# Smaller projection pieces, x prefetched by groups, and partial row sums on VectorE in entry 0 of a two-layer graph attention kernel

## Chip, cores and metric

The kernel runs on one core of a Trainium2 chip. The metric is the device time of one execution in microseconds; the median of several runs is compared.

## What is computed

Eight graphs (entries) of 2,048 nodes with 256 features share one adjacency matrix. Layer 0 is an attention layer with eight heads of 32 features, whose scores are sums of a source and a destination term with a leaky ReLU, plus a logarithmic prior made from the adjacency. Layer 1 is a dot-product attention layer with one head. Each has a residual and a layer norm.

```
# layer 0, per entry
x_proj = einsum('bnd,hdf->bhnf', x, W)
e = leaky_relu(e_src[..., :, None] + e_dst[..., None, :], 0.2)
e = where(adj > 0, e + softplus(beta_tilde) * log(adj + 1e-6), -max)
h = einsum('bhij,bhjf->bhif', softmax(e), x_proj)     # then @ W_out.T
x = layernorm(x + h)
# layer 1
e = where(adj > 0, leaky_relu((x W1)(x W2)^T, 0.2), -1e12)
x = layernorm(x + relu(softmax(e) (x W3)))
```

## The kernel before

**Layer 0 as units.** The exponential of a leaky ReLU of a sum is the larger of two products, so no exponential is taken per score. For one pair of heads (`hp`, 0 to 3) and one tile of 128 keys (`jt`, 0 to 15), a *unit*, `step` (line 295) makes for each of the two heads one tile `s` of 128 keys x 2,048 queries by one VectorE instruction (line 311): the maximum of a query row `c`, broadcast over the partitions, and a per-key number, times the transposed mask `mt`. TensorE then multiplies `s` by the projected values into `val` and by a per-key weight, broadcast to 32 columns, into `den`, the row sums of the softmax (`products`, line 333). `s` has four buffers, that is two units.

**Row sums on VectorE.** `SUMMED` (line 67) lists key tiles whose row sums aren't taken by `den` matmuls. The first of a list is scaled by ScalarE into two tiles `d` (line 324), one for each head; the others are added to them by VectorE (line 318), a unit later in program order; at the last key tile one group of matmuls with ones adds `d` to `den` (line 329). Entry 0's list is empty before the change.

**Entry 0.** Its 64 units run alone, before layer 1 of any entry. In its first pair (units 0 to 15) the masks are made: `make_mt` (line 163) loads a column block of the adjacency as `adj_t`, makes `m` by VectorE (line 168), two ScalarE passes (169, 170) and VectorE again (171), transposes it on TensorE (176), copies it out on ScalarE (177) and stores it as `mt_d`. `m` has the two buffers of tag "p". Masks are made one tile ahead of their unit. The later pairs load `mt` back, with two buffers of tag "mt" and two of tag "d".

**Projections as filler.** Entry 0's own projection comes first. Those of entries 1 to 7 (`project`, line 225) are cut into pieces and put between entry 0's units by the main loop (lines 479 to 483). There are six pieces for each entry: four groups of 512 rows, each with the transposes of the next group ahead of it (`turn`, line 234), one piece for the scaling of the values `v` (line 270, a VectorE instruction of 4,096 elements), and one for `est` (line 277), from which the rows `c` are made. x is loaded in halves of 1 MB into the buffers of tag "p", which the masks use too. `later_weights` (line 133) prepares W_out, W1 W2 and W3, with a buffer of tag "pen".

**The end of a pair.** `finish` (line 341) copies `val` and `den` out on ScalarE, moves one row of each quarter of `den` into `rc` by DMA, takes the reciprocal on VectorE (line 354), stores it, and after each second pair loads it back broadcast as `rb` and multiplies (line 363). Then the output projection (`y`, line 376) can start.

**Order.** TensorE's order is the program's. The other engines' order is chosen by a scheduler at compile time; each then works its queue in that order. All DMAs are issued by SyncE from one queue, also in a fixed order. After entry 0's units, layer 1 of an entry runs together with layer 0 of the next; nothing in the change touches that part.

Of the kernel before, what the change touches and what calls it, by code (L numbers as in the profile page):

```python
# [9 lines left out]
F32 = mybir.dt.float32  # L10
# [8 lines left out]
P = 128  # L19
# [8 lines left out]
def kernel(  # L28
# [26 lines left out]
    nc = tc.nc  # L55
    B, N, D = x.shape
    H, _, DH = w_proj.shape
    NT = N // P
    KC = D // P
    BK = 512  # L60
    NB = N // BK
    HALF = N // 2
    HP = 2
    NP = H // HP
    IG = BK // P

    SUMMED = [(), (1, 3, 6, 9, 12)] + [(1, 3, 6, 8, 11, 13)] * (B - 2)

    const = ctx.enter_context(tc.tile_pool(name="const", bufs=1))
    dram = ctx.enter_context(tc.tile_pool(name="dram", bufs=1, space=DRAM))  # L70
# [1 line left out]
    wide = ctx.enter_context(tc.tile_pool(name="wide", bufs=2))  # L72
# [5 lines left out]
    def mm_tile(name):  # L78
        return ps.tile([P, BK], F32, tag="mm", name=name)

    def wide_tile(name, tag, bufs, dtype=F32):
        return wide.tile([P, N], dtype, tag=tag, name=name, bufs=bufs)
# [6 lines left out]
    ident = const.tile([P, P], F32)  # L89
# [14 lines left out]
    nc.vector.scalar_tensor_tensor(beta[:, 3:4], beta[:, 0:1], 0.0, beta[:, 2:3], ALU.max, ALU.add)  # L104
    beta_c = beta[:, 3:4]

    def load_x(b, half):
        xr = wide.tile([P, NT // 2, D], F32, tag="p", name="xr", bufs=2)
        nc.sync.dma_start(xr, x[b].rearrange("(t p) d -> p t d", p=P)[:, ts(half, NT // 2), :])
        return xr  # L110

    first_x = [load_x(0, half) for half in range(2)]


    wp = const.tile([P, KC, D + 2 * H], F32)
# [17 lines left out]
    def later_weights():  # L133

        nc.sync.dma_start(w3s, w3.rearrange("(k p) d -> p k d", p=P))
        w1t, w2t = (chunk.tile([P, KC, D], F32, tag="pt", name=name, bufs=2) for name in ("w1t", "w2t"))
        for w, dst in ((w_out, wot), (w1, w1t), (w2, w2t)):
            src = wide.tile([P, KC, D], F32, tag="pen", name="square", bufs=1)
            nc.sync.dma_start(src, w.rearrange("(k p) c -> p k c", p=P))
            yield  # L140
            for kc in range(KC):
                t = mm_tile("sq_t")
                for o in range(KC):
                    nc.tensor.transpose(t[:, ts(o, P)], src[:, o, ts(kc, P)], ident)
                nc.scalar.copy(dst[:, kc, :], t[:, 0:D])
        yield
        for dc in range(KC):
            t = mm_tile("w12p")
            for kc in range(KC):
                nc.tensor.matmul(t[:, 0:D], w1t[:, kc, ts(dc, P)], w2t[:, kc, :], start=(kc == 0), stop=(kc == KC - 1))  # L150
            nc.scalar.copy(w12[:, dc, :], t[:, 0:D])
        yield
# [7 lines left out]
    rec_d = dram.tile([B, NP, 4, HALF], F32, name="rec_d")  # L160
    x1_d = dram.tile([B, N, D], F32, name="x1_d")

    def make_mt(jt):

        a = wide.tile([P, NT, P], I32, tag="d", name="adj_t", bufs=2)
        nc.sync.dma_start(a, adj[:, ts(jt, P)].rearrange("(t p) j -> p t j", p=P))
        m = wide.tile([P, NT, P], F32, tag="p", name="m", bufs=2)
        nc.vector.tensor_scalar(m, a, 0.0, None, ALU.max)
        nc.scalar.activation(m, m, AF.Ln, bias=eps_prior)
        nc.scalar.activation(m, m, AF.Exp, scale=beta_c)  # L170
        nc.vector.scalar_tensor_tensor(m, a, 0.0, m, ALU.is_gt, ALU.mult)
        mt = wide_tile("mt", "mt", 2)
        for g in range(NB):
            t = mm_tile("mtp")
            for k in range(IG):
                nc.tensor.transpose(t[:, ts(k, P)], m[:, g * IG + k, :], ident)
            nc.scalar.copy(mt[:, ts(g, BK)], t)
        nc.sync.dma_start(mt_d[ts(jt, P), :], mt)
        return mt
# [32 lines left out]
    def row_tile(name, bufs=4):  # L212
        return small.tile([P, D], F32, tag="row", name=name, bufs=bufs)


    class Gat:


        def __init__(self, b):
            self.b = b  # L220
            self.units = ((hp, jt) for hp in range(NP) for jt in range(NT))
            self.hts = []
            self.mts = []

        def project(self):


            b = self.b
            kept = "v" if b == 0 else ("h3", "x1t")[b % 2]
            self.v = v = whole.tile([P, NT, D], F32, tag=kept, name="v")  # L230
            both = small.tile([P, NT, 2 * H], F32, name="both", bufs=1)
            xrs, xts = [], []

            def turn(g):
                if g % 2 == 0:
                    xrs.append(load_x(b, g // 2) if b > 0 else first_x[g // 2])
                xt = chunk.tile([P, KC, BK], F32, tag="ht", name="xt", bufs=3)
                for kc in range(KC):
                    t = mm_tile("tr")
                    for k in range(IG):  # L240
                        nc.tensor.transpose(t[:, ts(k, P)], xrs[-1][:, g % 2 * IG + k, ts(kc, P)], ident)
                    nc.scalar.copy(xt[:, kc, :], t)
                xts.append(xt)

            turn(0)
            for g in range(NB):
                if g + 1 < NB:
                    turn(g + 1)
                for k in range(IG):
                    it = g * IG + k  # L250
                    t = mm_tile("proj")
                    for kc in range(KC):
                        nc.tensor.matmul(t[:, 0:D + 2 * H], xts[g][:, kc, ts(k, P)], wp[:, kc, :],
                                         start=(kc == 0), stop=(kc == KC - 1))
                    nc.scalar.copy(v[:, it, :], t[:, 0:D])
                    nc.scalar.copy(both[:, it, :], t[:, D:D + 2 * H])
                yield
            top = small.tile([P, 2, H], F32, name="top", bufs=1)
            ed, es = both[:, :, 0:H], both[:, :, H:2 * H]
            nc.vector.tensor_reduce(top[:, 0, :], ed.rearrange("p t h -> p h t"), AX.X, ALU.max)  # L260
            nc.gpsimd.partition_all_reduce(top[:, 1, :], top[:, 0, :], P, bass_isa.ReduceOp.max)
            cs = small.tile([P, H, NT], F32, name="cs", bufs=1)
            nc.vector.tensor_tensor(cs, es.rearrange("p t h -> p h t"),
                                    top[:, 1, :].unsqueeze(2).to_broadcast([P, H, NT]), ALU.add)
            nc.vector.tensor_tensor(ed, ed, top[:, 1:2, :].to_broadcast([P, NT, H]), ALU.subtract)
            self.re = re = small.tile([P, 2, NT, H], F32, name="re", bufs=2)
            nc.scalar.activation(re[:, 0], ed, AF.Exp, scale=-(1.0 - ALPHA))
            nc.scalar.activation(re[:, 1], ed, AF.Exp)
            v4 = v.rearrange("p t (h f) -> p (t h) f", f=DH)
            nc.vector.tensor_tensor(v4, v4, re[:, 1].rearrange("p t h -> p (t h)").unsqueeze(2).to_broadcast(  # L270
                [P, NT * H, DH]), ALU.mult)
            if b > 0:
                nc.sync.dma_start(v_d[b], v)
                nc.sync.dma_start(re_d[b], re)
            yield
            t = mm_tile("est")
            nc.tensor.transpose(t[:, 0:P], cs.rearrange("p h t -> p (h t)"), ident)
            est = row_tile("est")[:, 0:P]
            nc.scalar.activation(est, t[:, 0:P], AF.Exp, scale=1.0 - ALPHA)
            nc.sync.dma_start(c_d[b].rearrange("h (t p) -> (h t) p", p=P), est)  # L280
            yield
# [13 lines left out]
        def step(self, count=1):  # L295

            for _ in range(count):
                hp, jt = next(self.units)
# [3 lines left out]
                    self.den = pacc.tile([P, HALF], F32, tag="den", name="den")  # L302
                first = self.b == 0 and hp == 0
                while first and len(self.mts) < min(jt + 2, NT):
                    self.mts.append(make_mt(len(self.mts)))
                mt = self.mts[jt] if first else load_mt(jt, self.b == 0)
                s = []
                for a in range(HP):
# [3 lines left out]
                    s.append(sa)  # L312
                v, e = self.v, self.re[:, 1]
                heads = [hp * HP + a for a in range(HP)]
                chain = SUMMED[self.b]
                if jt - 1 in chain[1:]:
                    for d, sa, h in zip(self.sums, self.last, heads):
                        nc.vector.scalar_tensor_tensor(d, sa, e[:, jt - 1, h:h + 1], d, ALU.mult, ALU.add)  # L318
                self.last = s
                self.products(self.val, [v[:, jt, ts(h, DH)] for h in heads], s, jt == 0, jt == NT - 1)  # L320
                if jt in chain[:1]:
                    self.sums = [wide_tile("d", "d", 2) for _ in heads]
                    for d, sa, h in zip(self.sums, s, heads):
                        nc.scalar.activation(d, sa, AF.Copy, scale=e[:, jt, h:h + 1])
                if jt not in chain:
# [149 lines left out]
    for _ in gats[0].project():  # L475
        pass
    others = (1 for g in gats[1:] for _ in g.project())
    weights = later_weights()
    pieces = (B - 1) * (NB + 2)
    for k in range(NP * NT):  # L480
        gats[0].step()
        for _ in range((k + 1) * pieces // (NP * NT) - k * pieces // (NP * NT)):
            next(others)
        if k >= NT and k % 4 == 0:
            next(weights, None)
    for _ in others:
        pass


    dot = None  # L490
    for b in range(1, B + 1):
# [53 lines left out]
```

## Time and profile before

| | us |
|---|---|
| median of 3 runs | 4469.75 |
| lowest, highest | 4466.98, 4470.57 |
| span of the profiled execution | 4465.4 |
| PE, DVE, ACT busy in it | 4267.6, 3631.8, 1758.7 |
| entry 0's own projection and first masks | 0 to 41 |
| s of units 0 to 15 (pair 0, masks made) | 53.9 to 209.2 |
| s of units 16 to 63 (pairs 1 to 3) | to 535.1 |
| first output matmul (y) | 559.3 |

PE is TensorE, DVE VectorE, ACT ScalarE, SP SyncE. A group of instructions is given by line, engine, operation and tiles, with its count, its busy time, the mean duration of one in ns, and then the idle time of the engine just before such instructions with the work that ended it. A row of waits reads: engine and line that waited, the engine and line waited for, total, number, longest. Each fp32 matmul appears in the records as two instructions.

### The profile page before, as it was taken

Reading aid. Unit: us, or ns where it says so; the run is one execution under the profiler, and the core shown is the slowest. Engines: PE = TensorE matmul, PEld = TensorE weight load, DVE = VectorE, ACT = ScalarE, POOL = GpSimd, SP = SyncE. Lnnn points to the kernel's source line nnn. Section 1 sums busy time; section 2 is a strip of 40 time slices with the busy share of each in tenths; the row PEclk is TensorE's granted clock in tenths of the full one; section 3 lists DMA queues with packets and bytes.
Section 4 is the critical chain, followed back from the end, with each engine's and each line's share of the span. In section 5 each row is a group of like instructions: output and inputs, shape, how many; then the busy total and the mean of one; then the engine's idle time right before and its main releaser. Section 6 shows DMA issues by size and latency. Waiting matters only on the chain.

```text
span 4465.4 us, 60558 instructions
## 1 busy us (share of the span) xinstructions
PE 4267.6 (96%) x24988; PEld 2217.3 (50%) x24988; DVE 3631.8 (81%) x2605; ACT 1758.7 (39%) x3611; POOL 7.5 (0%) x14
## 2 busy tenths in 40 slices
PE   6899899999999999999999999999999999999899
PEld 4444344445455545555455544545454554554566
DVE  5778798888989988988899888888988888898222
ACT  5622233334333343334333343333433343333555
POOL 0000000000000000000000000000000000000000
PEclk8999999999999999999999999999999999999999
DMA  7777665666555555556555565555545565553211
GB/s 217 262 264 263 249 218 204 220 233 217 180 189 193 182 193 184 188 181 224 176 182 178 186 213 187 189 181 207 194 160 190 189 216 183 187 182 134 69 50 41
DMA packets 252773, 843.62 MB, mean 189 GB/s; under 512 B 33616, under 2 KB 152400, under 8 KB 176976
## 3 DMA queue, kind: packets, MB, share of 16 engines
q1 hardware_dynamic: 252496, 839.74, 54.0%
q8 instruction: 196, 3.21, 0.3%
q14 instruction: 81, 0.66, 0.0%
HBM read 763.76 MB, written 75.37 MB: 188 GB/s over the span
## 4 chain that ended last, share of the span: by engine, by line
PE 60%; DVE 14%; issue 8%; ACT 4%; DMA 1%; SPq 0%; DVEq 0%; ACTq 0%
PE acc L461 17%; PE e L426 15%; PE val L336 12%; DVE s L311 9%; PE den L336 8%; PE pt L445 4%; DVE d L318 3%; PE h1p L416 2%; ACT p L432 1%; PE h3p L396 1%; ACT h L210 1%; DVE p L431 1%; PE y L376 1%; DMA mt<-mt_d 0%; ACT f L206 0%
## 5 line engine op out<-in xcount | busy, mean ns | idle before, releaser
L311 DVE SCALAR_TENSOR_TENSOR s<-c,re,mt 128x2048 f32<-128x2048 f32 x1024 | 2350.6, 2343 | 209.6 <-PE den L336 159.9
L336 PE MATMUL val<-s,v 128*32 128x512 f32 x8192 | 1045.3, 607 | 78.7 <-DVE s L311 78.5
L461 PE MATMUL acc<-h,pts 128*128 128x256 f32 x4096 | 950.6, 380 | 14.9 <-ACT pts L447 14.4
L426 PE MATMUL e<-x1t,h 128*128 128x512 f32 x2048 | 904.0, 594 | 0.0
L461 PEld LDWEIGHTS acc<-h,pts 128*128 128x128 f32 x4096 | 748.2, 190 | 107.7 <-ACT pts L447 21.8
L336 PE MATMUL den<-s,re 128*32 128x512 f32 x5568 | 709.2, 598 | 0.0
L318 DVE SCALAR_TENSOR_TENSOR d<-s,re,d 128x2048 f32<-128x2048 f32 x272 | 632.4, 2343 | 0.0
L426 PEld LDWEIGHTS e<-x1t,h 128*128 128x128 f32 x2048 | 379.6, 190 | 450.1 <-issue 417.9
L336 PEld LDWEIGHTS val<-s,v 128*32 128x32 f32 x8192 | 240.9, 110 | 697.8 <-issue 526.3
L447 ACT COPY pts<-pt 128x512 f32<-128x512 f32 x512 | 296.1, 583 | 664.7 <-PE pt L445 664.4
L428 ACT ACTIVATE p<-e 128x512 f32<-128x512 f32 x512 | 302.5, 595 | 432.3 <-PE e L426 432.3
L431 DVE CUSTOM_DVE_ANT_0 p<-p,pen 128x2048 f32<-128x2048 f32 x128 | 292.7, 2287 | 205.9 <-ACT p L428 205.6
L336 PEld LDWEIGHTS den<-s,re 128*32 128x32 f32 x5568 | 194.2, 112 | 426.7 <-issue 426.6
L432 ACT ACTIVATE p<-p,neg 128x2048 f32<-128x2048 f32 x128 | 256.7, 2005 | 272.5 <-DVE neg L431 272.5
L445 PEld LDWEIGHTS pt<-ident,p 128*128 128x128 f32 x2048 | 238.0, 141 | 223.5 <-issue 167.2
L445 PE MATMUL pt<-ident,p 128*128 128x128 f32 x2048 | 318.7, 279 | 5.4 <-ACT p L432 5.4
L469 DVE TENSOR_TENSOR z<-z,x1r 128x256 f32<-128x256 f32 x128 | 54.0, 422 | 205.4 <-ACT z L468 197.0
L468 ACT ACTIVATE z<-acc,rec 128x256 f32<-128x256 f32 x128 | 60.6, 473 | 355.9 <-PE acc L461 330.3
L376 PE MATMUL y<-wot,ht 128*128 128x256 f32 x512 | 129.6, 414 | 37.4 <-DVE ht L363 36.3
L206 ACT ACTIVATE f<-mv,eps_ln 128x1 f32<-128x1 f32 x256 | 74.2, 290 | 199.0 <-DVE mv L204 198.1
L396 PE MATMUL h3p<-w3s,x1t 128*128 128x256 f32 x512 | 133.4, 386 | 12.3 <-ACT x1t L392 12.3
L376 PEld LDWEIGHTS y<-wot,ht 128*128 128x128 f32 x512 | 104.7, 208 | 68.3 <-DVE ht L363 39.2
(76 smaller groups left out, 2083.6 us busy)
## 6 DMA issues: line engine op xcount, KB each, us to landing
mt<-mt_d SPq DMA_DIRECT2D x496, 1024.0 KB, 4.8
c<-c_d SPq DMA_DIRECT2D x64, 1024.0 KB, 6.7
pen<-pen_d SPq DMA_DIRECT2D x112, 512.0 KB, 3.3
xr<-in_x_dram SPq DMA_DIRECT2D x16, 1024.0 KB, 7.1
adj_t<-in_adj_dram SPq DMA_DIRECT2D x16, 1024.0 KB, 6.8
mt_d<-mt SPq DMA_DIRECT2D x16, 1024.0 KB, 5.6
rb<-rec_d SPq DMA_DIRECT2D x64, 256.0 KB, 4.0
h<-in_x_dram SPq DMA_DIRECT2D x32, 512.0 KB, 5.9
```

The lines of the kernel that those rows point to most:

```text
L311: nc.vector.scalar_tensor_tensor(sa, self.cs[a], self.re[:, 0, jt, h:h + 1], mt, ALU.max, ALU.mult)
L318: nc.vector.scalar_tensor_tensor(d, sa, e[:, jt - 1, h:h + 1], d, ALU.mult, ALU.add)
L336: nc.tensor.matmul(dst[ts(q, DH), ts(c, BK)], weights[q % 2], s[q % 2][:, ds(q // 2 * HALF + c * BK, BK)], start=start, stop=stop)
L376: nc.tensor.matmul(y[:, 0:D], ht[:, ts(it, P)], wot[:, g, :], start=(g == 0), stop=(g == 1))
L396: nc.tensor.matmul(t[:, 0:D], x1t[:, kc, ts(it - 1, P)], w3s[:, kc, :], start=(kc == 0), stop=(kc == KC - 1))
L426: nc.tensor.matmul(t, self.h1[:, kc, ts(it % IG, P)], self.x1t[:, kc, ts(c, BK)], start=(kc == 0), stop=(kc == KC - 1))
L428: nc.scalar.activation(p[:, ts(c, BK)], t, AF.Prelu, alpha=ALPHA)
L431: nc.vector.tensor_tensor_reduce(p, p, pen, -1.0, FMAX, ALU.add, ALU.min, neg)
L432: nc.scalar.activation(p, p, AF.Exp, bias=neg, scale=-1.0, accum_out=den)
L445: nc.tensor.transpose(t[:, ts(k, P)], p[:, ts(g * IG + k, P)], ident)
L447: nc.scalar.copy(pt, t)
L461: nc.tensor.matmul(acc, now[:, ts(k, P)], self.h3[:, j, :], start=(j == 0), stop=(j == NT - 1))
```

## The change

It does four things. Entry 0's pairs 1 to 3 get a list of six summed key tiles. The projection pieces become one row tile of 128 rows each, 18 for each entry, spread over the first 60 of the 64 units, so that the filler is even and ends before the last units. x is loaded in groups of 512 rows (0.5 MB) into the single buffer of tag "pen", each when the transposes of the group before have been queued; a group is thus a group ahead of its use, and tag "p" is left to `m` and, in pairs 1 to 3, to the sums `d`. And `m` is made one tile further ahead of its transposes. The weights' loads move to row buffers.

```diff
-    SUMMED = [(), (1, 3, 6, 9, 12)] + [(1, 3, 6, 8, 11, 13)] * (B - 2)
+    SUMMED = [(1, 3, 6, 8, 11, 13), (1, 3, 6, 9, 12)] + [(1, 3, 6, 8, 11, 13)] * (B - 2)
...
-            src = wide.tile([P, KC, D], F32, tag="pen", name="square", bufs=1)
-            nc.sync.dma_start(src, w.rearrange("(k p) c -> p k c", p=P))
+            src = [row_tile("square") for _ in range(KC)]
+            for o in range(KC):
+                nc.sync.dma_start(src[o], w[ts(o, P), :])
...
+    def x_groups():
+
+        for b in range(1, B):
+            for g in range(NB):
+                xg = wide.tile([P, IG, D], F32, tag="pen", name="xg", bufs=1)
+                nc.sync.dma_start(xg, x[b].rearrange("(t p) d -> p t d", p=P)[:, ts(g, IG), :])
+                yield xg
+
+    groups = x_groups()
+    ahead = []
...
             def turn(g):
-                if g % 2 == 0:
-                    xrs.append(load_x(b, g // 2) if b > 0 else first_x[g // 2])
+                if b == 0:
+                    xr = first_x[g // 2][:, ds(g % 2 * IG, IG), :]
+                else:
+                    xr = ahead.pop() if ahead else next(groups)
...
+                if b > 0:
+                    ahead.extend(xg for xg in [next(groups, None)] if xg is not None)
 
             turn(0)
-            for g in range(NB):
-                if g + 1 < NB:
+            for it in range(NT):
+                g, k = divmod(it, IG)
+                t = mm_tile("proj")
+                for kc in range(KC):
+                    nc.tensor.matmul(t[:, 0:D + 2 * H], xts[g][:, kc, ts(k, P)], wp[:, kc, :],
+                                     start=(kc == 0), stop=(kc == KC - 1))
+                nc.scalar.copy(v[:, it, :], t[:, 0:D])
+                nc.scalar.copy(both[:, it, :], t[:, D:D + 2 * H])
+                if k == 0 and g + 1 < NB:
                     turn(g + 1)
...
                 while first and len(self.mts) < min(jt + 2, NT):
-                    self.mts.append(make_mt(len(self.mts)))
+                    at = len(self.mts)
+                    while len(self.ms) < min(at + 1 + (jt > 0), NT):
+                        self.ms.append(make_m(len(self.ms)))
+                    self.mts.append(make_mt(at, self.ms[at]))
...
-                chain = SUMMED[self.b]
+                chain = () if first else SUMMED[self.b]
...
-                    self.sums = [wide_tile("d", "d", 2) for _ in heads]
+                    self.sums = [wide_tile("d", "d" if self.b else "p", 2) for _ in heads]
...
-    pieces = (B - 1) * (NB + 2)
+    pieces = (B - 1) * (NT + 2)
     for k in range(NP * NT):
         gats[0].step()
-        for _ in range((k + 1) * pieces // (NP * NT) - k * pieces // (NP * NT)):
+        due = [min(i * pieces // (NP * NT - 4), pieces) for i in (k, k + 1)]
+        for _ in range(due[1] - due[0]):
             next(others)
-        if k >= NT and k % 4 == 0:
+        if k >= NT and k % 4 == 2:
             next(weights, None)
-    for _ in others:
-        pass
-
```

More of the change, by code (lines that the diff above doesn't have):

```diff
@@ L105 @@
     beta_c = beta[:, 3:4]
[L107 to L112, printed above, removed]
+    first_x = [wide.tile([P, NT // 2, D], F32, tag="p", name="xr", bufs=2) for _ in range(2)]
+    for half, xr in enumerate(first_x):
+        nc.sync.dma_start(xr, x[0].rearrange("(t p) d -> p t d", p=P)[:, ts(half, NT // 2), :])
     wp = const.tile([P, KC, D + 2 * H], F32)
@@ L143, in later_weights @@
                 for o in range(KC):
-                    nc.tensor.transpose(t[:, ts(o, P)], src[:, o, ts(kc, P)], ident)
+                    nc.tensor.transpose(t[:, ts(o, P)], src[o][:, ts(kc, P)], ident)
                 nc.scalar.copy(dst[:, kc, :], t[:, 0:D])
@@ L161, with make_m @@
     x1_d = dram.tile([B, N, D], F32, name="x1_d")
-    def make_mt(jt):
+    def x_groups():
[6 more added lines that the diff above has]
+    ahead = []
+    def make_m(jt):
         a = wide.tile([P, NT, P], I32, tag="d", name="adj_t", bufs=2)
@@ L171, in make_mt @@
         nc.vector.scalar_tensor_tensor(m, a, 0.0, m, ALU.is_gt, ALU.mult)
+        return m
+    def make_mt(jt, m):
         mt = wide_tile("mt", "mt", 2)
@@ L222, in __init__ @@
             self.hts = []
-            self.mts = []
+            self.ms, self.mts = [], []
         def project(self):
@@ L231, in project @@
             both = small.tile([P, NT, 2 * H], F32, name="both", bufs=1)
-            xrs, xts = [], []
+            xts = []
             def turn(g):
-                if g % 2 == 0:
-                    xrs.append(load_x(b, g // 2) if b > 0 else first_x[g // 2])
+                if b == 0:
+                    xr = first_x[g // 2][:, ds(g % 2 * IG, IG), :]
+                else:
+                    xr = ahead.pop() if ahead else next(groups)
                 xt = chunk.tile([P, KC, BK], F32, tag="ht", name="xt", bufs=3)
@@ L240, in turn @@
                     for k in range(IG):
-                        nc.tensor.transpose(t[:, ts(k, P)], xrs[-1][:, g % 2 * IG + k, ts(kc, P)], ident)
+                        nc.tensor.transpose(t[:, ts(k, P)], xr[:, k, ts(kc, P)], ident)
                     nc.scalar.copy(xt[:, kc, :], t)
                 xts.append(xt)
+                if b > 0:
+                    ahead.extend(xg for xg in [next(groups, None)] if xg is not None)
             turn(0)
-            for g in range(NB):
-                if g + 1 < NB:
-                    turn(g + 1)
[L249 to L256, printed above, removed]
+            for it in range(NT):
[7 more added lines that the diff above has]
+                if k == 0 and g + 1 < NB:
+                    turn(g + 1)
                 yield
```

## The prediction

> **What bounds the kernel now.** The change touches only entry 0's attention. From the first query-product matmul of layer 1 on (633 us) the compiled program queues the same instructions in the same order on all engines, so I read the first 560 us. First the slices of the page, for the shape:
>
> ```profile
> PE   6899899999999999999999999999999999999899
> DVE  5778798888989988988899888888988888898222
> ```
>
> A slice is 111.6 us. In the first five TensorE is less full than later, and VectorE is not full either. Then the busy time by stretch: pair 0, where the masks are built (unit 15's s end at 209.2); pairs 1 to 3 (unit 63's s end at 535.1); the passage into the next stage.
>
> ```profile
> core 0: us, PE busy (x) PEld busy (x) DVE busy (x) ACT busy (x) POOL busy (x), PEclk, DMA share, GB/s
> 41.00:209.00 168.00, 131.72 (x916) 74.68 (x916) 130.12 (x67) 108.92 (x170) 0.36 (x1) 0.91 0.81 260
> 209.00:535.00 326.00, 295.08 (x2057) 131.79 (x2057) 253.92 (x125) 74.16 (x242) 6.03 (x6) 0.96 0.71 256
> 535.00:560.00 25.00, 13.75 (x82) 3.58 (x83) 13.08 (x8) 6.47 (x6) 0.00 (x0) 0.73 0.84 293
> ```
>
> Nobody is saturated in pairs 1 to 3; PE looks nearer the bound, but its 295 us hold cold stretches. The waits of the second stretch say why:
>
> ```profile
> DVE s L311 <- PE den L336: 56.6, 21, 4.4
> DVE s L311 <- PE proj L253: 6.7, 1, 6.7
> DVE s L311 <- DMA c<-c_d: 2.9, 2, 2.6
> ...
> PE val L336 <- DVE s L311: 29.9, 14, 5.2
> ```
>
> Both wait for each other: VectorE some 66 us, TensorE 30. The four s buffers hold two units, and a projection lump is longer than that slack, as PE's timeline shows (start, duration):
>
> ```profile
> 490.11 1.99 PE L241 MATMUL tr<-ident,xr 128*128 128x128 f32 x16
> 491.94 3.93 PE L253 MATMUL proj<-wp,xt 128*128 128x272 f32 x16
> 495.80 1.92 PE L336 MATMUL val<-s,v 128*32 128x512 f32 x16
> 497.54 1.90 PE L336 MATMUL den<-s,re 128*32 128x512 f32 x16
> 499.38 1.09 PE L241 MATMUL tr<-ident,xr 128*128 128x128 f32 x8
> ```
>
> From start to start: four row tiles of projection 3.86, val 1.74, den 1.84, one group's transposes 0.92. What VectorE does in 209.5 to 535.1:
>
> ```profile
> L311 DVE SCALAR_TENSOR_TENSOR s<-c,re,mt 128x2048 f32<-128x2048 f32 x96 | 220.1, 2346 | 66.2 <-PE den L336 56.6 <-PE proj L253 6.7 <-DMA c<-c_d 2.9
> L270 DVE TENSOR_TENSOR v<-v,re 128x4096 f32<-128x4096 f32 x6 | 26.5, 4423 | 2.5 <-ACT re L268 2.5
> L363 DVE TENSOR_TENSOR ht<-ht,rb 128x2048 f32<-128x2048 f32 x1 | 2.3, 2283 | 0.0
> ```
>
> With the four small groups (cs 2.2, top 2.1, both 1.7, rc 1.0) that is 255.9 us of 325.6.
>
> In pair 0 the mask chain costs most: VectorE waits from 63 us on are
>
> ```profile
> DVE s L311 <- ACT mt L177: 13.2, 4, 4.7
> DVE m L168 <- PE mtp L176: 12.2, 4, 3.9
> DVE m L168 <- DMA adj_t<-in_adj_dram: 5.4, 2, 5.1
> ```
>
> **What the Trainium skill says.** (1) "VectorE: DVE Perf Modes", section "The perf-mode tier table": an fp32 operation on two tensors has only the 1x mode, 2,293 ns for 2,048 elements. Lines 311 and 318 agree, 2.29 to 2.35 us; a cheaper add on VectorE isn't to be had. (2) "TensorE: Matmul & The Clock Gate", section "What's actually happening": an array that idled for about 3.4 us runs at half rate. The trace agrees: after a 3 us wait at 292 us eleven val matmuls take 2.78 us, against 1.49 at 535 us. (3) "DMA: Bandwidth & Descriptors", section "Anatomy of one DMA": a semaphore wait happens on the issuing sequencer, not in the DMA engine. So an x load that waits for TensorE holds up mt loads behind it on SyncE; no row of the trace shows such a block by itself.
>
> **Part 1, the row sums.** Per pair six of sixteen tiles lose their den matmuls, and one group with ones comes back: 3 x (6 - 1) x 1.8 = 27 us off TensorE. The first tile of each pair is scaled on ScalarE, 6 x 2.0 = 12 us; it is busy 74 of 326 us, so hidden, but a projection copy can stand behind it for 2 to 4 us. The other five are added on VectorE: 3 x 5 x 2 = 30 adds. The row for this very operation,
>
> ```profile
> L318 DVE SCALAR_TENSOR_TENSOR d<-s,re,d 128x2048 f32<-128x2048 f32 x272 | 632.4, 2343 | 0.0
> ```
>
> gives 632.4/272 = 2.325 us, so 69.7 us. VectorE then needs 255.9 + 69.7 = 325.6 us for a stretch that lasts 325.6 us now. This is the step that carries the forecast: pairs 1 to 3 can't become shorter, and each microsecond of VectorE idleness left in them is lost.
>
> **Part 2, pieces of a row tile.** 126 pieces over 60 units, 2.1 per unit: TensorE's extra per unit is 2.1 x 0.96 + 0.5 x 0.92 = 2.5 us instead of lumps of 4.8. A plain unit then costs it 3.6 + 2.5 = 6.1 us and VectorE 4.6; a summed unit 4.3 against 9.2. Of the 66 us of waits for TensorE the smoothing and the lighter den remove most. What stays, by estimates:
> - Start of a pair (three times): the second c row can't be loaded before the last unit's first s has read its buffer; c lands in 6.7 us (issue table), with two s (4.6 us) to hide it: 2 to 2.9 us, 7 in all.
> - From unit 14 of a pair to unit 3 of the next no add falls due. TensorE has two plain units, the ones, two more plain units and a summed one before VectorE is delayed again, some 29 us against 23, with 4.6 us of lead; and the reciprocal (line 354) stands after two units of the next pair in VectorE's queue, with all later s behind it, and waits for the later-closing den. 3 us twice: 6.
> - x a group ahead with one buffer: at an entry's start turn(0), one projection and turn(1) are one piece. The load for turn(1) goes out when turn(0) has read the buffer, lands in about 6 us (h, same 512 KB, 5.9 in the issue table), and TensorE has 1 us of work: it stands still for 5 us, and val, the next mask transposes and all else on PE behind it. Five times in pairs 1 to 3. VectorE is then a unit ahead and has just got the 4.4 us of v, so it loses from 0 to 5 us, I take 1.2: 6.
> - Cold stretches after such waits: 3.
> Sum 22 us; from 8 (all but the c rows hidden) to 38 (stalls not hidden, mt loads late).
>
> **Part 3, masks one tile deeper (pair 0).** x no longer takes turns with m in the "p" buffers, and m is made a tile further ahead; the 12.2 and part of the 13.2 us go. VectorE's floor per unit is 4.6 + 2.3 + 1.2 = 8.1 us, with v 8.5; ScalarE has 4.0 + 2.3 + 1.7 = 8.0 and TensorE 3.6 + 1.9 + 2.5 = 8.0. Three engines this close won't run at 8.5; I take 9.2, where units 3 to 15 now take 123.4/12 = 10.3: gain 13. Against it: the first piece now lies before the transposes of mask 2, with its 5 us of waiting for x, so unit 3 starts about 4.5 us later (85.7 instead of 81.2), and entry 2's start in unit 9 costs up to 6, taken as 4. Net gain 5 us, from a loss of 5 to a gain of 15.
>
> **Part 4, the passage.** Today
>
> ```profile
> 546.02 0.35 DVE L354 RECIPROCAL rc<-rc 128x32 f32<-128x32 f32 x1 [10.97 <-DMA rc<-dn]
> ```
>
> holds four s of the next entry behind it. The changed queue puts these ahead of the reciprocal, and the last four units carry no projection. VectorE gains 9 us, but the output matmuls still wait for den, rc, rb and the product of line 363, 24 us after unit 63, and den closes 1.9 us later with the ones. I take 3 us, from 0 to 6. The weights' new buffers and slots cost nothing: the same 20 small matmuls (4 us) lie in TensorE's slack.
>
> Sum: 22 - 5 - 3 = +14 us, 4484.
>
> **Rivals.**
> *No change:* stalls are absorbed (8 to 12) and pair 0 gains 8 to 10. For it: TensorE, 295 - 27 = 268 us busy of 326, will have 58 us of slack in pairs 1 to 3 to catch up in. Against: VectorE has none. 10 - 8 - 3 = -1, about 4469.
> *Faster:* pair 0 runs near its floor (-15), the passage gives 5, and pairs 1 to 3 lose only 4: -16, 4454. For it: the 25 us of mask waits are of the kind that one tile more of depth removes. Against: three engines within half a microsecond of one another.
> *Much slower:* SyncE's queue makes mt late after each x load (5 x 3 more), pair 0 gains nothing: 22 + 15 - 2 = +35, 4505.
>
> **Numbers.** Main case 0.42, much slower 0.10, no change 0.28, faster 0.20. Low end 4455, high end 4506. Slower by over 0.2% (8.9 us) takes the first two.
>
> **What would show it.** Over pairs 1 to 3 VectorE should be busy about 325 us in a stretch of 335 to 360; TensorE's waits for s should exceed VectorE's for den. Each entry's turn(1) should show a wait for xg of some 5 us. The reciprocal should wait for its transfer. Unit 3's s should start near 86 us. I am wrong if that stretch is below 333 us, if adds cost less than 2.2 us each, or if pair 0 ends before 195 us.

## The result, and the profile after

The changed kernel takes 4487.03 us (median of 4 runs, 4485.46 to 4488.95) against 4469.22 us: a ratio of 1.0041, 95% interval 1.0023 to 1.0058. It is slower by 17.8 us; 4484 was forecast. The span of the profiled execution is 4487.2 us, 21.8 more than before. Every trace is one execution, and executions of one kernel lie up to 12 us apart here, so a few us between two traces mean little by themselves.

Lines of `kernel.py` have moved: s is line 331 (311 before), the add 338 (318), val and den 356 (336), the transposes of x 257 (241), the reciprocal 374 (354), the product with rb 383 (363). Where the text says "the stretch" of a run, it means pairs 1 to 3, from the end of unit 15's s to the end of unit 63's s. Below, "later turn" means that the transposes of the next x group stand two pieces later.

The slices of the changed kernel's page, PE above DVE:

```profile
PE   6888889999999999999999999999999999999899
DVE  5799998888989988888998888888988888898222
```

VectorE is now at 90% or more in the third to sixth slice, and TensorE has gone down there: the bound has changed sides. The same stretches as before the change (pair 0 and pairs 1 to 3):

```profile
core 0: us, PE busy (x) PEld busy (x) DVE busy (x) ACT busy (x) POOL busy (x), PEclk, DMA share, GB/s
41.00:207.00 166.00, 137.18 (x923) 76.99 (x921) 132.47 (x69) 110.38 (x177) 0.77 (x2) 0.89 0.79 250
207.00:555.00 348.00, 292.47 (x1802) 129.93 (x1800) 319.70 (x155) 86.77 (x249) 11.95 (x6) 0.92 0.71 248
```

Pairs 1 to 3 went from 325.9 to 348.5 us. VectorE's busy time in them rose from 253.9 to 319.7 us, by about 66, and its idle time fell by about 44, from 72 to 28; the balance is the growth of the stretch, 22.6 us. Marks on the way, from VectorE's timeline and the first matmul of layer 1 (h1p):

| | before, us | after, us | difference added |
|---|---|---|---|
| s of unit 0 starts | 53.9 | 56.6 | +2.7 |
| s of unit 15 ends | 209.2 | 207.1 | -4.8 |
| s of unit 63 ends | 535.1 | 555.6 | +22.6 |
| first h1p | 633.3 | 653.4 | -0.4 |
| end | 4465.4 | 4487.2 | +1.7 |

What VectorE did most in pairs 1 to 3 of the changed kernel, by group:

```profile
L331 DVE SCALAR_TENSOR_TENSOR s<-c,re,mt 128x2048 f32<-128x2048 f32 x97 | 222.5, 2342 | 19.3 <-DMA mt<-mt_d 8.8 <-DMA c<-c_d 5.4 <-PE den L356 2.9
L338 DVE SCALAR_TENSOR_TENSOR d<-s,re,d 128x2048 f32<-128x2048 f32 x30 | 69.5, 2343 | 0.0
```

The 56.6 us of waits for den have become 2.9, and 69.5 us of adds have taken their place. The waits there, VectorE's and then TensorE's:

```profile
DVE s L331 <- DMA mt<-mt_d: 8.8, 2, 4.5
DVE s L331 <- DMA c<-c_d: 5.4, 3, 2.6
DVE rc L374 <- DMA rc<-dn: 3.6, 2, 2.6
DVE top L277 <- ACT both L271: 3.6, 3, 2.5
DVE s L331 <- PE den L356: 2.9, 3, 1.7
DVE s L331 <- PE val L356: 2.1, 1, 2.1
...
PE val L356 <- DVE s L331: 23.2, 19, 3.9
PE tr L257 <- DMA xg<-in_x_dram: 17.3, 5, 5.7
PE est L294 <- DVE cs L280: 13.9, 4, 4.1
```

TensorE now waits for VectorE (23.2 and 13.9 us); VectorE's waits for den and val are down to 5.0. The five waits for xg are the starts of the five entries whose projection begins in these pairs: turn(1) has nothing to hide its load behind. In pair 0 TensorE waits for xg twice, 3.0 and 3.1 us, with mask transposes behind it. VectorE's waits from 63 to 207 us:

```profile
DVE m L178 <- PE mtp L190: 23.1, 5, 10.7
DVE s L331 <- ACT mt L191: 3.8, 2, 2.8
```

The waits of s for mt fell from 13.2 to 3.8 us, those of m for the transposes rose from 12.2 to 23.1, of which two, of 10.7 and 10.6 us, lie right after the starts of entries 1 and 2; the later turn (below) halves these waits, to 11.2 us. At the passage

```profile
568.46 0.35 DVE L374 RECIPROCAL rc<-rc 128x32 f32<-128x32 f32 x1 [1.97 <-DMA rc<-dn]
```

comes after four s, where it held them for 10.97 us before.

### The profile page after: what moved, and what is told of

Same layout as the page of the kernel before. It is cut to its first block, busy times and chain, and to the rows that moved or that the text cites. A ratio compares the mean times of both kernels' runs of the same rounds, so it can differ in the third digit from the quotient of the medians.

```text
span 4487.2 us, 60148 instructions
## 1 busy us (share of the span) xinstructions
PE 4272.2 (95%) x24748; PEld 2219.9 (49%) x24748; DVE 3698.2 (82%) x2635; ACT 1772.0 (39%) x3617; POOL 13.4 (0%) x14
## 3 DMA queue, kind: packets, MB, share of 16 engines
q1 hardware_dynamic: 252768, 839.74, 53.9%
## 4 chain that ended last, share of the span: by engine, by line
PE 59%; DVE 15%; issue 8%; ACT 4%; DMA 2%; SPq 0%; DVEq 0%
PE acc L481 16%; PE e L446 15%; PE val L356 11%; DVE s L331 10%; PE den L356 8%; PE pt L465 4%; DVE d L338 3%; PE h1p L436 2%; PE y L396 1%; ACT p L452 1%; PE h3p L416 1%; DVE p L451 1%; ACT h L224 1%; DMA mt<-mt_d 1%; DVE ht L383 0%
## 5 line engine op out<-in xcount | busy, mean ns | idle before, releaser
L338 DVE SCALAR_TENSOR_TENSOR d<-s,re,d 128x2048 f32<-128x2048 f32 x302 | 702.0, 2343 | 0.0
L356 PE MATMUL den<-s,re 128*32 128x512 f32 x5280 | 670.3, 598 | 0.0
L356 PEld LDWEIGHTS den<-s,re 128*32 128x32 f32 x5280 | 184.9, 112 | 404.4 <-issue 402.2
L344 ACT ACTIVATE d<-s,re 128x2048 f32<-128x2048 f32 x62 | 124.3, 2005 | 75.1 <-DVE ht L383 62.2
L268 PE MATMUL proj<-wp,xt 128*128 128x272 f32 x512 | 142.7, 420 | 11.8 <-DVE wp L125 8.2
```

Source lines behind the costliest of these rows:

```text
L356: nc.tensor.matmul(dst[ts(q, DH), ts(c, BK)], weights[q % 2], s[q % 2][:, ds(q // 2 * HALF + c * BK, BK)], start=start, stop=stop)
```

## Experiments

**Which part costs the time.** Four kernels, with one edit each of the changed kernel, or two.

```diff
-    SUMMED = [(1, 3, 6, 8, 11, 13), (1, 3, 6, 9, 12)] + ...
+    SUMMED = [(), (1, 3, 6, 9, 12)] + ...
```

> The changed kernel with entry 0's list of summed tiles empty again; all else as changed. Theory A (VectorE is full in pairs 1 to 3 because of the 30 adds): VectorE's busy time there falls from 320 to 254 us, TensorE takes its 27 us of den matmuls back and is the bound at 272 us of work plus 17 us of waits for x, so the stretch from unit 15 to unit 63 falls from 348 to 295 to 315 us and the total to about 4444 (4430 to 4455), below the kernel before. Theory B (the loss comes from the waits for x and from the order of the queues, the adds are hidden): the stretch stays above 335 us and the total within 10 us of 4487.

4464.1 us, ratio to the kernel before 0.9991 (0.9982 to 0.9999). Without the list the stretch is 20 us shorter and the total 23, so theory B is out; but theory A's size was missed as well (4444). Pairs 1 to 3 by busy time:

```profile
206.70:535.00 328.30, 295.47 (x2057) 130.22 (x2056) 254.80 (x126) 74.62 (x243) 10.00 (x6) 0.95 0.73 261
```

and the waits there, VectorE's ahead of TensorE's:

```profile
DVE s L331 <- PE den L356: 58.0, 37, 5.1
...
PE tr L257 <- DMA xg<-in_x_dram: 15.8, 5, 3.8
PE est L294 <- DVE cs L280: 7.8, 6, 4.6
PE val L356 <- DVE s L331: 7.1, 3, 3.4
```

TensorE is the bound: 295 us of busy time and 31 of waits. I had priced its work at full clock (272 us); the records hold 295, with half-rate stretches after waits for x. The sixteen val records last 3.62 us here, 1.92 at full rate:

```profile
238.22 1.94 PE L257 MATMUL tr<-ident,xg 128*128 128x128 f32 x8 [3.37 <-DMA xg<-in_x_dram]
240.09 3.62 PE L356 MATMUL val<-s,v 128*32 128x512 f32 x16
```

So the small pieces as the change has them show no gain in these pairs (328.3 against 325.9, in an execution 4.7 us above the kernel's median): what smoothing gives, the wait for x takes, as the fourth run shows.

```diff
-                if k == 0 and g + 1 < NB:
+                if k == 2 and g + 1 < NB:
                     turn(g + 1)
```

> The changed kernel with the transposes of the next x group put two pieces later (after the third row tile of a group instead of the first), sums kept. The load of group 1 then has about one unit to land. Theory A: TensorE's 17 us of waits for xg in pairs 1 to 3 vanish, but VectorE is full, so that stretch gains only what VectorE idled for it, 0 to 10 us (mt transfers queued behind x 8.8 us); in pair 0 VectorE's two waits of 10.6 us for the mask transposes shrink to under 4 us each, 10 to 16 us. Total 4468 (4460 to 4478). Theory B: both the x waits in pair 0 and all 17 us in pairs 1 to 3 count, and the delays behind them: about 4448 (4440 to 4458).

4470.59 us, 1.0007 (0.9998 to 1.0015): theory A. Pair 0 (first s to the end of unit 15) takes 136.0 us instead of 150.5; unit 15 ends at 196.4, 10.7 us earlier. In pairs 1 to 3 TensorE's waits for xg fall from 17.3 to 3.4 us, and the stretch only from 348.5 to 342.8:

```profile
196.40:539.20 342.80, 289.58 (x1801) 125.24 (x1800) 319.81 (x155) 86.18 (x249) 11.95 (x6) 0.95 0.71 253
```

TensorE's longest sum of waits there:

```profile
PE val L356 <- DVE s L331: 33.1, 26, 3.8
```

TensorE waits 33 us for s instead of 23: most of the time that it no longer loses on x it waits for VectorE.

```diff
-    SUMMED = [(1, 3, 6, 8, 11, 13), (1, 3, 6, 9, 12)] + ...
+    SUMMED = [(1, 6, 11), (1, 3, 6, 9, 12)] + ...
```

> The changed kernel with three summed tiles (1, 6, 11) for each pair of entry 0 instead of six: 12 adds instead of 30. Theory A: VectorE's work in pairs 1 to 3 falls by 18 x 2.2 = 40 us to 280, TensorE's rises by 9 x 1.8 = 16 us; VectorE still bounds by little, so the stretch falls to 300 to 318 us and the total to about 4450 (4440 to 4462). Theory B: no more than 10 us below 4487.

4475.29 us, 1.0014 (1.0008 to 1.0021). Between the two theories, and neither's number. By the medians three tiles cost 11 us against none, with the turn where the change has it. The traces don't show where: pairs 1 to 3 take 327.3 us, one less than with no sums, but this execution lay 4.8 us below its kernel's median and the other 4.7 above. TensorE is busy for 13 us less than with no sums; one of its waits for xg is 10.4 us here, and all five add up to 23.1 instead of 15.8.

The next kernel has both the empty list and `k == 2`.

> Both of the edits of the first two runs: no sums in entry 0 and the transposes of the next x group two pieces later. Theory A: with VectorE no longer full, TensorE's 17 us of waits for x do count in pairs 1 to 3, unlike with the sums: that stretch falls by 10 to 17 us below that of the run without sums, to about 288, and pair 0 gains 10 to 16 us as well; total about 4420 (4408 to 4432). Theory B: as the second run, 4448 to 4470.

4438.99 us, 0.9933 (0.9916 to 0.9949), faster than the kernel before by 30 us, though not by the 49 expected. Pairs 1 to 3 by busy time:

```profile
198.60:509.50 310.90, 291.54 (x2058) 128.32 (x2056) 254.25 (x126) 74.18 (x243) 10.00 (x6) 0.97 0.76 276
```

The later turn takes 17.4 us off these pairs where VectorE has room (328.3 to 310.9) and 5.7 us where it is full (348.5 to 342.8). By the totals it is 25.1 and 16.4 us, of which 8.1 and 10.7 come from pair 0. That difference is the test of "VectorE is full": where VectorE has room, taking away 15.8 us of waits for xg shortens the stretch by at least as much; where it is full, taking away 13.9 us gives 5.7.

**How many tiles, and do masks and pieces matter.** All with the later turn.

```diff
+    SUMMED = [(1, 6, 11), (1, 3, 6, 9, 12)] + ...      # three tiles
```

> Three summed tiles (1, 6, 11) for each of entry 0's pairs 1 to 3, with the later turn. Without sums and with the later turn pairs 1 to 3 took 310.9 us with TensorE the bound, with six tiles 342.8 us with VectorE full. Theory A (balance): VectorE 254 + 12 x 2.2 = 280 us, TensorE 3 x 2 x 1.8 = 11 us less; the stretch falls to 298 to 308 us and the total to about 4431 (4424 to 4438), the fastest so far. Theory B (any add on VectorE disturbs more than a den group costs TensorE, since adds come in lumps of 4.5 us): no better than 311 us, total 4439 to 4452.

4455.19 us, 0.9966 (0.9953 to 0.9979): theory A failed, and the total is 3 us above theory B's range too. Pairs 1 to 3 take 319.6 us.

```diff
+    SUMMED = [(1, 8), (1, 3, 6, 9, 12)] + ...          # two tiles
```

> Two summed tiles (1, 8) for each pair, with the later turn: the first is scaled on ScalarE, so there are only 6 adds (13 us of VectorE), and TensorE saves 3 x 1 x 1.8 = 5 us. Theory A (balance): stretch 303 to 309 us, total about 4435, between no sums and three tiles. Theory B (adds disturb): 311 to 318 us, total 4439 to 4446.

4436.51 us, 0.9924 (0.991 to 0.9939), with a stretch of 308.1 us. That is the number of theory A, but two tiles can't be told from none: the intervals of the totals overlap, and another run with no sums (the next one) has the same 308.1 us. The two stretches, three tiles above two:

```profile
197.10:516.70 319.60, 285.92 (x1945) 125.79 (x1944) 280.11 (x137) 85.69 (x249) 11.96 (x6) 0.96 0.74 266
```

```profile
197.40:505.50 308.10, 287.78 (x1993) 126.93 (x1992) 267.00 (x131) 85.56 (x249) 13.91 (x6) 0.97 0.76 278
```

The longer list adds 13.1 us to VectorE, 11.5 to the stretch and 18.7 to the total, while VectorE's idle time stays at some 40 us. Of the 11.5 us, 8.8 lie in one pair (units 32 to 47: 112.4 us against 103.6), which holds one wait of 7.0 us for mt and one of 5.7 us for xg. Why the order of transfers came out so with that list isn't settled, and the two lists name different tiles, not only one more; the balance of busy times alone does not pick the number of tiles.

The next two kernels have no sums either.

```diff
-                    while len(self.ms) < min(at + 1 + (jt > 0), NT):
+                    while len(self.ms) < min(at + 1, NT):
```

> No sums, later turn, and the masks m made no further ahead than in the kernel before (one tile ahead of their unit); x stays out of the p buffers. Theory A (the depth is what pair 0 gains from): the waits for the mask chain return, VectorE idles some 25 us for mt and mtp in pair 0, which takes 10 to 20 us longer than the 136.7 us (first s to end of unit 15) of the run with depth: total 4449 to 4459. Theory B (x leaving the p buffers alone did it): within 4 us of 4439.

4439.45 us, 0.9932 (0.9915 to 0.9948), against 4438.99 with the depth. Pair 0 takes 136.0 us against 136.7. Theory B: with this turn and these pieces the depth of the masks does nothing measurable.

```diff
-                yield
+                if k == IG - 1:
+                    yield
...
-    pieces = (B - 1) * (NT + 2)
+    pieces = (B - 1) * (NB + 2)
```

> No sums, later turn, but the pieces are again lumps of four row tiles, six pieces for each entry, over the first 60 units. Theory A (the size of the piece set the mutual waiting of VectorE and TensorE in the kernel before): the stretch of pairs 1 to 3 goes back from 310.9 to 322 to 332 us (325.6 before the change) and pair 0 loses a few us more: total 4452 to 4465. Theory B (the order of x and the masks did it, not the size of the pieces): within 5 us of 4439.

4467.98 us, 0.9997 (0.9989 to 1.0006): theory A, with a total 3 us above its range. The waits are close to those of the kernel before (61.6 us of VectorE for den, 28.7 of TensorE for s). By busy time:

```profile
203.90:535.60 331.70, 296.29 (x2053) 129.97 (x2052) 253.71 (x125) 74.64 (x241) 2.20 (x6) 0.95 0.70 255
```

And the lumps with the six sums:

> The run with lumps of four row tiles and the later turn, plus the six summed tiles of the change: the sums in an arrangement like that of the kernel before, where VectorE idled 62 us for den in pairs 1 to 3 (331.7 us in all). Theory A (VectorE's 320 us of work are a floor whatever the pieces, and some 25 us of pair starts and transfers remain): 342 to 352 us, total 4478 to 4490, so the sums cost 10 to 20 us here too. Theory B (the adds slip into the idle time that the lumps make, and den leaves TensorE's long units shorter): no more than 334 us, total at most 4470.

4478.96 us, 1.0023 (1.0015 to 1.0031). Pairs 1 to 3:

```profile
204.60:544.70 340.10, 280.89 (x1797) 124.48 (x1796) 320.20 (x155) 86.06 (x247) 8.05 (x6) 0.92 0.70 251
```

This makes a square, us of pairs 1 to 3, all with the later turn:

| | no sums | six tiles |
|---|---|---|
| lumps of four row tiles | 331.7 | 340.1 |
| pieces of one row tile | 310.9 | 342.8 |

The stretch was just under the 342 to 352 expected, and the total inside its range: theory A. VectorE's 320 us are the floor in both cells on the right, and there the piece's size makes no difference that favours small pieces. In the left column it is worth 20.8 us. Read by rows, the sums cost 8.4 us with lumps and 31.9 with pieces. With lumps VectorE idled 78 us, and most of the 66 us of adds went into that time; with pieces it idled 57, and about half of them did. Some 20 to 23 us of idle time are left in both cells on the right, so the sums save nothing in either row.

**What holds up mt.** VectorE's 8.8 us of waits for mt were not in the main case of the prediction.

```diff
-                nc.sync.dma_start(xg, ...)
+                nc.gpsimd.dma_start(xg, ...)
```

> The changed kernel, with the x groups of entries 1 to 7 issued by GpSimd instead of SyncE; all else as changed. In pairs 1 to 3 VectorE waits 8.8 us for mt transfers. Theory A (an x load that waits for TensorE at the head of SyncE's queue holds up the mt loads behind it, the price that the prediction put at the late end): the waits for mt fall to 2 us or less, the stretch from 348 to 339 to 344 us, the total to 4479 (4474 to 4483). Theory B (mt is held up by stores that wait for VectorE, of the reciprocals and of v): waits for mt stay at 6 us or more, the total between 4483 and 4491. The waits of TensorE for xg stay at about 17 us under both.

4500.62 us, 1.0071 (1.0056 to 1.0086), outside the ranges of both theories: slower by another 14 us. The mt waits fell only to 5.3 us, and TensorE's waits for xg grew, against the 17 us that I had expected to stay:

```profile
PE tr L257 <- DMA xg<-in_x_dram: 23.8, 5, 7.1
```

A group takes 5.3 us from issue to landing here (median in pairs 1 to 3), 4.5 on SyncE's queue.

```diff
-                nc.sync.dma_start(v_d[b], v)
-                nc.sync.dma_start(re_d[b], re)
+                nc.gpsimd.dma_start(v_d[b], v)
+                nc.gpsimd.dma_start(re_d[b], re)
...
-            nc.sync.dma_start(rec_d[b, hp]...., rc)
+            nc.gpsimd.dma_start(rec_d[b, hp]...., rc)
```

> The changed kernel, with the stores of v, re and the reciprocals (all entries) issued by GpSimd instead of SyncE; x stays on SyncE. Theory B (these stores, which wait for VectorE and ScalarE, hold up mt): the waits for mt in pairs 1 to 3 fall from 8.8 to 2 us or less and the total to 4479 (4472 to 4483). Theory A (x holds up mt): waits for mt stay at 6 us or more, total 4483 to 4491.

4484.94 us, 1.0034 (1.0022 to 1.0046), not to be told from the changed kernel by the total. The waits for mt are 3.8 us, one instead of two, and the stretch is 344.6 us. That is between the two theories, and neither kind of transfer alone is shown to cause these waits.

SyncE's own waits, which the prediction did not read, show that several kinds of transfer do hold its queue. In pairs 1 to 3 of the changed kernel it stood 39.9 us at x loads for the transposes that free their buffer (17 times, 6.6 us at most), 47.8 us at the stores of v and re, and 112.2 us at the mt loads themselves, for an s that frees theirs. Which of them makes a particular mt late stays open. The waits also change without any move between queues: with all transfers on SyncE and six sums they are 8.8 us in the changed kernel, 5.5 with the later turn and 0.2 with the lumps.

**The parts that helped, together.** Two tiles, later turn, masks not further ahead, those stores on GpSimd:

> Two summed tiles, later turn, masks no further ahead than before the change, and the stores of v, re and the reciprocals issued by GpSimd: the parts that helped, together. Under theory B of the other two runs the 8.5 us of waits for mt go: pairs 1 to 3 take 299 to 304 us (308.1 with two tiles and later turn), total about 4429 (4423 to 4435). Under theory A nothing is gained: 4434 to 4440.

4429.05 us, 0.9907 (0.9891 to 0.9924): 40 us below the kernel before and 58 below the changed one. Pairs 1 to 3 by busy time, and VectorE's largest wait in them:

```profile
198.60:498.70 300.10, 284.99 (x1993) 126.95 (x1992) 266.77 (x131) 85.64 (x249) 22.09 (x21) 0.98 0.78 284
```

```profile
DVE s L331 <- PE den L356: 28.2, 19, 2.8
```

No wait for mt is left, TensorE's clock is at 0.98, and it is busy for 285 of 300 us. Against the run with two tiles this one has two edits, the stores and the masks. Its four times (4425.9 to 4430.1 us) all lie below the four of that run (4435.5 to 4437.4), though the intervals of the ratios overlap: together the edits seem worth some 7 us. What each is worth isn't shown, all the less since the masks' edit alone, with no sums, took the mt waits from 7.6 to 2.7 us.

## Why the prediction was right

**The sums (part 1): right.** "Pairs 1 to 3 can't become shorter" held: VectorE has 320 us of busy time in every run with six tiles, and none of them took under 340 us in these pairs. The adds' 69.7 us are 69.5 in the group's row; since neighbouring records overlap a little (two s of 2.35 us last 4.61 together), they added 66 to the busy time. TensorE's 27 us did not appear as shorter busy time: it has 255 records fewer, but was busy for 292.5 us instead of 295.1, at a granted clock of 0.92 instead of 0.96. The 268 us that the rival "no change" counted on were not there.

**The idle time that stays (part 2): the growth of the stretch is right, 22 forecast and 22.6 measured, but by two errors that cancel.** VectorE's busy time came out 6 us lower than the 325.6 reckoned, which adds groups as if none overlapped, and its idle time 6 higher, 28 instead of 22. That the two are equal is luck. By term: c rows 7 forecast, 5.4 measured; start of a pair and reciprocal 6, against 3.6 for rc and 5.0 for val and den; x stalls 5 us each, measured 3.5 on average (17.3 in five), and their price 6, measured 5.7 by taking most of them away. (The prediction gives TensorE some 29 us from unit 14 to unit 3; its own prices add up to 30.5, and only then do its 3 us come out.)

The 3 us for cold stretches have no row of their own: of the five waits for xg with no sums, those of 3.06 us and more were followed at once by half rate (1.94 us for eight transposes), the one of 2.72 us was not (1.06); 3.06 us is a little less than the 3.4 us that the prediction names. Missing were 3.6 us of waits for ScalarE's copies at line 277, which stands ahead of s in VectorE's queue and needs the last row tile, and 8.8 us for mt. The latter had been given to the rival "much slower", with x loads at the head of SyncE's queue as cause; moving x to another queue left 5.3 us of them, so that cause isn't shown.

**Pair 0 (part 3): a smaller gain, and one of its two causes wrong.** Unit 3 started at 89.9 us (85.7 forecast), because the first s was already 2.7 us late, and the stall for x (3.0 us) with the projections and mask transposes after it kept VectorE idle for 10.7 us. The units after it took 9.4 us each with entry 2's stall in them (9.2 and 4 us once, that is 9.5). Unit 15 ended 2.1 us earlier, 5 had been forecast. The step "the 12.2 and part of the 13.2 us go" named two causes, x out of the masks' buffers and m a tile further ahead. The waits of m for the transposes grew, to 23.1 us; those of s for mt did fall. And the depth isn't a cause: with the later turn nothing is lost without it. What helped must be among the other things that changed there, x out of the masks' buffers and in smaller groups, or the smaller pieces. Unit 15 ends at 209.2 us before the change, at 203.9 with lumps and the later turn, and at 196.4 to 198.6 with pieces and the later turn: about half of it comes without the small pieces. (Counted from the first s it looks like more, 155.3, 142.7 and 136.0 us, but with the later turn the first s starts 7 us later than before.) Since no run has x back in those buffers, that it is the buffers was only argued.

**The passage (part 4): 3 us forecast, 0.4 found.** VectorE did run ahead by four s, as foreseen, but the first h1p follows unit 63 by 97.8 us, 98.2 before: the output matmuls waited for the product of line 383 to the end, so VectorE's lead had nobody to help:

```profile
584.15 8.69 PE L396 MATMUL y<-wot,ht 128*128 128x256 f32 x30 [9.21 <-DVE ht L383]
```

**The rivals.** "Faster" leaned on pair 0 near its floor and on absorbed stalls; pair 0 does come near it (unit 15 ends at 196.4 us) once the turn stands later, but the change doesn't do that. "No change" needed TensorE's slack to absorb the stalls, 8 to 12 us left, and pair 0 to gain 8 to 10; the idle time was 28 us, and pair 0 gained 2.1.

## What to carry to other kernels

When work is moved from a fuller engine to another, write down for the stage in question the receiving engine's busy time plus the added work, and compare it with the stage's length: if they are equal, the other engine's savings can't appear. Two remedies for one imbalance aren't additive: here both use VectorE's idle time. Smaller filler pieces shortened the stretch by 20.8 us by reducing it, and six sums, which filled it, cost 8.4 us with lumps but 31.9 with small pieces. A prefetch "one group ahead" with one buffer is only ahead if other work stands between the release of the buffer and the next use; two pieces later was worth 16 to 25 us here, pair 0 included.

## What the runs showed that I had not expected

A list of three summed tiles is slower than one of two by about as much as its adds (11.5 us of the stretch for 13.1 us of work, 18.7 of the total), although VectorE idles some 40 us in both; why isn't known. Moving 0.5 MB loads from SyncE's queue to GpSimd's cost 14 us, with 5.3 instead of 4.5 us from issue to landing. And TensorE's busy time for the same matmuls goes from 295 us at a granted clock of 0.95 (no sums) to 289 us at 0.98 (no sums, later turn, masks not ahead), and half-rate stretches follow most of the waits for x (val 3.62 us instead of 1.92 after a wait of 3.37): such a stall cost more than its own length.
